# A graph attention kernel: self loops taken out of the edge lists, layer 2's sums split by columns between two engines, small tiles first

## The chip, the cores and the metric

The kernel runs on one core of a Trainium2 chip. The metric is the device time of one execution in microseconds (us), here the median of several runs. The profile comes from one more execution, taken by the hardware profiler. Engines are named as it names them: PE (matrix products; PEld loads their weights), DVE (vector engine), ACT (scalar engine), POOL (GpSimd), and SP, which here only issues transfers.

## What is computed

Two layers of graph attention over 10,000 nodes and 170,000 edges, then a final normalisation. All numbers are float32.

```python
src = concatenate([_s, _d, arange(10000)])      # 80000 random pairs, both ways, and one loop a node
dst = concatenate([_d, _s, arange(10000)])      # then both sorted by dst
def gat_conv(x, edge_index, W, a_src, a_dst, bias, heads, out_ch, concat):
    ei = _add_self_loops(edge_index, n)         # one more loop for every node
    xl = (x @ W).reshape(n, heads, out_ch)
    e = leaky_relu(alpha_src[src] + alpha_dst[dst], 0.2)
    e = exp(e - segment_max(e, dst)[dst])
    alpha = e / (segment_sum(e, dst)[dst] + 1e-16)
    return segment_sum(xl[src] * alpha[:, :, None], dst) + bias
h = relu(layer_norm(gat_conv(x, ..., heads=4, out_ch=256))) + (x @ Wr1 + br1)
h = layer_norm(gat_conv(h, ..., heads=1, out_ch=768)) + (h @ Wr2 + br2)
return layernorm(x + h)
```

The list of edges already holds a loop for each node, and the convolution adds another, so a node attends to itself twice.

## The kernel before, in words

There are three stages, and each handles the nodes in 79 tiles of 128, one node on each partition.

**Stage one** (lines 513 to 579) multiplies x by W1 tile by tile, adds each row's attention terms and writes it to a table in DRAM (`table1`, rows of 1032 numbers). In the same loop `prepare()` runs in small steps. It sorts the nodes by number of in-edges, most first, and builds `slots`: for tile t it has SLOTS[t] columns, each with one table row for every one of the tile's 128 nodes. `slot_counts()` (line 54) fixes these sizes ahead of the run, from the expected distribution of in-degrees with a margin of four standard deviations: `CAPS[t]` columns for the listed edges, and one in front for the added loop. A node with fewer edges gets the number of an empty row in the rest. If any tile had more edges than columns, `fits` would be zero and the program would take `general_path()`.

**Layer 1** (`ordered_layer1`, line 581) goes through the tiles from the most in-edges to the fewest. A `Ring` of 28 buffers is filled by indirect gathers on POOL (line 364), one a slot, 128 rows of 4 KB each. A gather into a buffer is issued once the slot before in that buffer has been consumed (`ring.fetch`, called after each slot). For a tile, `logits` (line 403) and `normalised` (line 420) turn the last columns of all its slots into softmax weights: small DVE operations with one exponential on ACT. The weighted rows are then summed into `acc` in PSUM, by three means:

- the first two slots (`ON_PE1`) by PE, with diagonal matrices that ACT makes from the weights (lines 616 to 629);
- of the others, every third by DVE alone, four operations of 256 columns (line 439);
- the rest by ACT, which multiplies the row in place (line 433), and DVE, which adds it in one operation of 1024 columns (line 435).

Between the slots of tile t stand the dense products: `deviation` and `scaled` (lines 468 and 480) normalise the sums of tile t-1 into h, `columns` (line 487) transposes h and x on PE, and `product` (line 145) multiplies h by W2 for layer 2's table, and x by Wr1 for the residual. The calls stand by hand: `events` has slot numbers at which `dense` and `next_x` are called. All PSUM results of products and transposes rotate through one pool of two buffers (`ps_big`). A tile with more slots than the ring has buffers (the first, 42) is done in three parts by `attend_parts` (line 442).

**Layer 2** (`ordered_layer2`, line 683) goes through the tiles in the same order, with rows of 770 numbers from `table2`, one head and a ring of 40. DVE alone sums the slots, one operation of 768 columns each (line 439). PE only makes the residual product (lines 740 and 742) from h1, which SP loads, and x, which POOL gathers. DVE normalises twice (lines 468 to 485 and 722 to 732), ACT does the last scaling (line 733), and POOL scatters the finished rows to the output (line 758). In each tile the steps stand in this order on DVE: the statistics and scaling of tile t-1, the weights of tile t, the final statistics of tile t-1, then the slots of tile t.

Each engine executes its own list of instructions in order, and waits where an operand isn't ready.

Of the kernel before, what the change touches and what calls it, by code (L numbers as in the profile page):

```python
# [26 lines left out]
F32 = mybir.dt.float32  # L28
# [5 lines left out]
P = 128  # L34
# [4 lines left out]
NO_NODE = 1 << 20  # L39
DEGREES = 64  # L40
# [3 lines left out]
RING2 = 40  # L44
ON_PE1 = 2
# [8 lines left out]
def slot_counts(n_nodes, n_edges):  # L54
# [8 lines left out]
    for t in range(-(-n_nodes // P)):  # L63
        room = t * P if t else 0.002
        k = next((k for k, m in enumerate(tails) if m + 4.0 * math.sqrt(m) * (t > 0) <= room), DEGREES - 3)
        counts.append(min(k + 1, DEGREES - 2))
# [4 lines left out]
def gnn_kernel(ctx, tc, x, x_cols, src, dst, src_col, dst_col, W1, a_src1, a_dst1, b1, g1, be1, Wr1, br1,  # L71
# [12 lines left out]
    SLOTS = [c + 1 for c in CAPS]  # L84
    FIRST = [sum(SLOTS[:t]) for t in range(NT)]
# [12 lines left out]
    ps_big = ctx.enter_context(tc.tile_pool(name="ps_big", bufs=2, space=PSUM))  # L98
    ps_tr = None

    @contextmanager
    def psum_for_transposes():

        nonlocal ps_tr
        with tc.tile_pool(name="ps_tr", bufs=2, space=PSUM) as ps_tr:
            yield
# [8 lines left out]
    slots = consts.tile([P, FIRST[-1] + SLOTS[-1]], I32, name="slots")  # L115
    order = consts.tile([P, NT], I32, name="order")
    fits = consts.tile([1, 1], I32, name="fits")
# [27 lines left out]
    def product(aT, w, n):  # L145

        k = w.shape[1]
        p = ps_big.tile([P, 2 * BANK], F32, name="big")
# [22 lines left out]
    def prepare():  # L171

        with tc.tile_pool(name="prep", bufs=1, side="right") as pool, \
# [144 lines left out]

            room = pool.tile([P, NT], F32, name="room")
            t = 0  # L320
            while t < NT:
                u = next((u for u in range(t, NT) if CAPS[u] != CAPS[t]), NT)
                nc.vector.memset(room[:, t:u], float(CAPS[t]))
                t = u
            nc.vector.tensor_sub(room, filled, room)
# [3 lines left out]
            yield  # L329
# [4 lines left out]


            def listed(t, window):
                k = CAPS[t]
                have = pool2.tile([P, CAPS[0]], F32, name="have")
                nc.vector.tensor_scalar(have[:, :k], node[:, :k], filled[:, t:t + 1], None, op0=OP.is_lt)
                got = pool2.tile([P, CAPS[0]], F32, name="got")  # L340
                nc.vector.tensor_scalar(got[:, :k], window[:, :k], float(-NP), None, op0=OP.add)
                nc.vector.tensor_mul(got[:, :k], got[:, :k], have[:, :k])
                nc.vector.tensor_scalar_add(slots[:, FIRST[t] + 1:FIRST[t] + 1 + k], got[:, :k], float(NP))
                nc.vector.tensor_copy(slots[:, FIRST[t]:FIRST[t] + 1], order[:, t:t + 1])

            asked = []
            for t in range(NT):
                k = CAPS[t]
                window = pool2.tile([P, CAPS[0]], I32, name="window", bufs=10)
                nc.gpsimd.indirect_dma_start(  # L350
                    out=window[:, :k], out_offset=None, in_=src,
                    in_offset=bass.IndirectOffsetOnAxis(ap=begin[:, t:t + 1], axis=0))
                asked.append((t, window))
                if t % 4 == 3:
                    for r in asked[:-4]:
                        listed(*r)
                    asked = asked[-4:]
                    yield
            yield
            for r in asked:  # L360
                listed(*r)
# [18 lines left out]
    class Ring:  # L380
# [6 lines left out]
        def fetch(self, upto):  # L387
            for q in range(self.issued, min(upto, FIRST[-1] + SLOTS[-1])):
# [31 lines left out]
    def normalised(small, e, heads):  # L420

        total = small.tile([P, heads], F32, name="total")
# [4 lines left out]

    def weigh(acc, row, e, dh, first=None, shared=False):

        if shared:  # L430
# [603 lines left out]
```

## Time and profile before

| what | us |
|---|---|
| median of 3 runs | 6468.38 (6455.11 to 6469.05) |
| profiled execution, its own time | 6474.16 |
| span in the profile | 6472.3 |
| DVE busy | 5053.9 (78%) |
| PE busy | 4198.2 (65%) |
| POOL busy | 3534.4 (55%) |
| ACT busy | 2688.0 (42%) |
| first gather of layer 1 at | 958.5 |
| first gather of layer 2 at | 3974.3 |

The profile gives the busy time of every engine, a table of the span in 40 equal slices, and groups of equal instructions with their number, their mean time and what ended the idle time before them. The trace behind it can be asked for any stretch: the instructions in order of time, the waits of an engine with what ended them, or a row of sums for a window. A line of the timeline has the start, the time taken, engine and line of code, operation, destination and sources, shapes and number, and in brackets the idle time before it with what ended it. The granted clock is PE's, as a share of full speed; the DMA share is the mean busy share of the core's 16 DMA engines. Issue times on POOL are about 0.95 us an indirect gather, with 0.30 between two.

### The profile page before, as it was taken

To read this page: it belongs to the slowest core of one execution; us is meant where nothing else is said; L and a number is where in the kernel's file an instruction comes from. 1 tells how busy PE (TensorE), PEld (TensorE's weight loads), DVE (VectorE), ACT (ScalarE), POOL (GpSimd) and SP (SyncE) were. 2 spreads that over 40 slices of the span, in tenths; PEclk is the share of its full clock that TensorE was granted. 3 is DMA by queue.
4 is the path that set the end of the run, shared out by engine and by line. 5 is a ranking of instruction groups with operands and counts; after the bars stand their busy time and mean duration, and the time that the engine had idled before them with its cause. 6 is when DMAs were issued, how large, how long until landed. Compare 5 with 4: busy or idle time off the path is not lost. (4 is left out here: it accounts for less than half of the span.)

```text
span 6472.3 us, 48744 instructions
## 1 busy us (share of the span) xinstructions
PE 4198.2 (65%) x11636; PEld 2278.5 (35%) x11636; DVE 5053.9 (78%) x8160; ACT 2688.0 (42%) x6591; POOL 3534.4 (55%) x3582
## 2 busy tenths in 40 slices
PE   8997982556766777778888996333434444445555
PEld 3443431333434444444455553111212222222332
DVE  5861426888888888888888884888878888888888
ACT  3433434666666666667666772011111111111111
POOL 3426534555555555555555553666666666666663
PEclk9999996778888888889899998666667777777777
DMA  4323237888888888888888885888878888888884
GB/s 140 122 76 70 93 106 287 289 293 315 299 301 301 303 304 297 300 295 299 293 299 307 308 312 180 277 281 288 281 272 287 282 280 281 279 286 283 279 291 161
DMA packets 459455, 1666.17 MB, mean 257 GB/s; under 512 B 105739, under 2 KB 109899, under 8 KB 459158
## 3 DMA queue, kind: packets, MB, share of 16 engines
q0 software_dynamic: 362176, 1486.59, 66.6%
q1 hardware_dynamic: 93168, 170.98, 7.8%
q10 hardware_dynamic: 3814, 5.39, 0.3%
q8 instruction: 94, 1.54, 0.1%
q14 instruction: 203, 1.66, 0.1%
HBM read 1516.88 MB, written 146.19 MB: 257 GB/s over the span
## 5 line engine op out<-in xcount | busy, mean ns | idle before, releaser
L364 POOL DMA_INDIRECT ring<-table,slots x2940 | 2789.2, 949 | 2161.4 <-DVE acc L439 889.7
L439 DVE SCALAR_TENSOR_TENSOR acc<-ring,e,acc 128x256 f32<-128x256 f32 (+1 forms) x3248 | 2332.4, 718 | 363.5 <-PE acc L625 201.5
L433 ACT ACTIVATE ring<-ring,e 128x256 f32<-128x256 f32 x3400 | 1390.8, 500 | 0.0
L435 DVE TENSOR_TENSOR acc<-acc,ring 128x1024 f32<-128x1024 f32 x850 | 1048.0, 1233 | 91.9 <-ACT ring L433 2.6
L740 PE MATMUL big<-wr,ident 128*128 128x512 f32 (+1 forms) x316 | 206.7, 745 | 1280.2 <-DMA wr<-in_x_dram,order 633.2
L742 PE MATMUL big<-w,wr 128*128 128x512 f32 (+1 forms) x2528 | 950.4, 531 | 23.1 <-issue 23.0
L625 PE MATMUL acc<-ring,diagonals 128*128 128x256 f32 x1248 | 424.3, 514 | 698.9 <-ACT diagonals L619 586.8
L152 PE MATMUL big<-w,hT 128*128 128x512 f32 (+1 forms) x2528 | 840.2, 490 | 56.8 <-ACT hT L494 56.8
L152 PE MATMUL big<-w,xT 128*128 128x512 f32 x1896 | 833.4, 601 | 55.8 <-DMA xT<-in_x_cols_dram 34.7
L152 PE MATMUL big<-wr,xT 128*128 128x512 f32 x1896 | 829.5, 594 | 0.7 <-ACT xT L494 0.7
L742 PEld LDWEIGHTS big<-w,wr 128*128 128x128 f32 x2528 | 531.3, 210 | 468.1 <-issue 432.6
L477 ACT ACTIVATE sd<-mv,eps 128x1 f32<-128x1 f32 x237 | 69.7, 294 | 1358.1 <-issue 585.4
L152 PEld LDWEIGHTS big<-w,hT 128*128 128x128 f32 x2528 | 471.9, 189 | 411.8 <-issue 289.1
L625 PEld LDWEIGHTS acc<-ring,diagonals 128*128 128x128 f32 x1248 | 326.9, 269 | 782.7 <-ACT diagonals L619 598.2
L152 PEld LDWEIGHTS big<-w,xT 128*128 128x128 f32 x1896 | 363.3, 193 | 522.9 <-issue 501.8
L740 PEld LDWEIGHTS big<-wr,ident 128*128 128x128 f32 x316 | 69.7, 249 | 1349.3 <-issue 449.3
L152 PEld LDWEIGHTS big<-wr,xT 128*128 128x128 f32 x1896 | 360.8, 190 | 423.4 <-issue 417.7
L417 ACT ACT_TABLE_LOAD x156 | 200.1, 1283 | 717.7 <-DVE e L416 636.7
L569 DVE TENSOR_TENSOR scr<-big,as_b 128x1024 f32<-128x1024 f32 x79 | 96.7, 1224 | 441.2 <-ACT row L566 426.3
L574 POOL TENSOR_TENSOR row<-row,none 128x1024 f32<-128x1024 f32 x79 | 187.0, 2368 | 334.9 <-ACT row L566 334.3
L572 ACT ACTIVATE scr<-scr 128x256 f32<-128x256 f32 x632 | 253.4, 402 | 122.2 <-DVE scr L569 118.3
L477 ACT ACT_TABLE_LOAD x157 | 201.4, 1283 | 229.7 <-DVE mv L475 149.5
(146 smaller groups left out, 3359.3 us busy)
## 6 DMA issues: line engine op xcount, KB each, us to landing
ring<-table,slots POOLq DMA_INDIRECT x2940
table<-row SPq DMA_DIRECT2D x79, 516.0 KB
h_d<-hT SPq DMA_DIRECT2D x79, 512.0 KB
wr<-h_d SPq DMA_DIRECT2D x79, 512.0 KB
xT<-in_x_cols_dram SPq DMA_DIRECT2D x79, 384.0 KB
w<-in_W_dram SPq DMA_DIRECT2D x6, 512.0 KB
w<-in_W_dram SPq DMA_DIRECT2D x1, 3072.0 KB
wr<-in_Wr_dram SPq DMA_DIRECT2D x1, 3072.0 KB
```

The costliest lines, as they stand in the source:

```text
L152: nc.tensor.matmul(p[:, c:e], aT[:, j, :], w[:, j, c:e], start=(j == 0), stop=(j == k - 1))
L364: nc.gpsimd.indirect_dma_start(out=to, out_offset=None, in_=table, in_offset=bass.IndirectOffsetOnAxis(ap=index, axis=0), **more)
L417: nc.scalar.activation(e, e, AF.Exp)
L433: nc.scalar.activation(row[:, s], row[:, s], AF.Copy, scale=e[:, h:h + 1])
L435: nc.vector.tensor_add(acc[:, :c], acc[:, :c], row[:, :c])
L439: nc.vector.scalar_tensor_tensor(acc[:, s], row[:, s], e[:, h:h + 1], (acc if first is None else first)[:, s], op0=OP.mult, op1=OP.add)
L477: nc.scalar.activation(sd, mv[:, 1:2], AF.Sqrt, bias=eps)
L572: nc.scalar.activation(m[:, s], m[:, s], AF.Copy, accum_out=row[:, C1 + i * H1 + h:C1 + i * H1 + h + 1])
L574: nc.gpsimd.tensor_add(row[:, :C1], row[:, :C1], b1_b)
L625: nc.tensor.matmul(acc[:, c:d], diagonals[:, k * H1 + i, :], ring.slot(FIRST[t] + k)[:, c:d], start=(k == 0 and c % BANK == 0), stop=(k == ...
L740: nc.tensor.matmul(r[:, c:d], ident, xt[:, c:d], start=True, stop=False)
L742: nc.tensor.matmul(r[:, c:d], hT[:, j, :], wr2[:, j, c:d], start=False, stop=(j == K1 - 1))
```

## The change

- The node's own loop is found in its list on the chip (`listed`) and taken out; the slot in front stands for both loops, and its weight is multiplied by `loops`, which is 2 where a loop was listed. A tile has one slot less.
- `slot_counts` uses a slightly smaller standard deviation.
- The tiles run from the fewest in-edges to the most, in both layers.
- Layer 1: of the rows after the first two, one in four and not one in three is summed by DVE alone (`SHARE`). The weights, diagonals and first two PE slots of tile t+1 are made during the last three slots of tile t (`LEAD`), where the ring can hold it. ACT's multiplication is issued three slots ahead. The pool `ps_big` becomes one buffer for the transposes and the product by W2, and one for the residual.
- Layer 2: DVE sums columns 0 to 511, and PE columns 512 to 767, into a PSUM tile of its own, with a diagonal from ACT for each slot. The weights are made ahead there too. Only the first tile's rows are asked for before the loads of biases and weights, and the product with br1 moves into the first tile.

The core of the diff (`prepare()` has the new lists first; the sizes, the order and the layers follow):

```diff
+BIG_SLOT = 4096.0
+LEAD = 3
+ON_PE2 = 512
+SHARE = 4
-        k = next((k for k, m in enumerate(tails) if m + 4.0 * math.sqrt(m) * (t > 0) <= room), DEGREES - 3)
+        k = next((k for k, m in enumerate(tails)
+                  if m + 4.0 * math.sqrt(m * (1.0 - m / n_nodes)) * (t > 0) <= room), DEGREES - 3)
-    SLOTS = [c + 1 for c in CAPS]
-    FIRST = [sum(SLOTS[:t]) for t in range(NT)]
+    SLOTS = CAPS
+    FIRST = [sum(SLOTS[t + 1:]) for t in range(NT)]
...
+            def listed(t, window):
+                m, k = window.shape[1:]
...
+                nc.vector.tensor_tensor(eq, window, named[:, t:t + m, None].to_broadcast(v), op=OP.is_equal)
+                nc.vector.tensor_mul(eq, eq, have)
+                nc.vector.tensor_mul(eq, eq, far[:, None, :k].to_broadcast(v))
+                nc.vector.tensor_reduce(loop[:, t:t + m], eq, axis=AX.X, op=OP.min)
...
+            nc.vector.tensor_scalar(loop, loop, 0.0, None, op0=OP.is_lt)
+            nc.vector.tensor_scalar_add(loops, loop, 1.0)
...
-    def normalised(small, e, heads):
+    def normalised(small, e, heads, t):
+        doubled(e, t)
...
+    def doubled(e, t):
+        nc.vector.tensor_scalar(e[:, 0], e[:, 0], loops[:, NT - 1 - t:NT - t], None, op0=OP.mult)
+    def multiply(row, e, dh):
+        for h in range(e.shape[1]):
+            s = slice(h * dh, (h + 1) * dh)
+            nc.scalar.activation(row[:, s], row[:, s], AF.Copy, scale=e[:, h:h + 1])
...
+    SLOTS, FIRST = SLOTS[::-1], FIRST[::-1]
...
     def ordered_layer1():
+                tc.tile_pool(name="ps_h1", bufs=1, space=PSUM) as ps_big, \
+                tc.tile_pool(name="ps_r1", bufs=1, space=PSUM) as ps_r, tc.manual_schedule():
             ring = Ring(pool, table1, R1, RING1)
-            ring.fetch(RING1)
+            ring.fetch(SLOTS[0])
...
+            def shared(k):
+                return (k - ON_PE1) % SHARE > 0
...
+                if full is not None:
+                    store(t - 2)
+                moves = []
+                if live:
+                    xT = pool.tile([P, K0, P], F32, name="xT")
+                    moves = columns(xT, xs[t])
+                multiplied(ON_PE1 + 2)
...
+                if whole and t + 1 < NT and SLOTS[t + 1] + LEAD <= ring.size:
+                    ahead = weights_of(t + 1)
+                for k in range(n if whole else 0):
+                    multiplied(k + 1 + LEAD)
+                    if k >= n - LEAD:
+                        ready += itertools.islice(ahead, 1)
+                    if k >= ON_PE1:
+                        weigh(acc, ring.slot(FIRST[t] + k), e[:, k], DH1, shared=shared(k))
+                    ring.fetch(FIRST[t] + k + 1 + ring.size)
+                    due(k)
...
     def ordered_layer2():
+            def sums(t, acc, e):
+                n = SLOTS[t]
+                nc.tensor.matmul(acc, ones, b2_b[0:1, ON_PE2:], start=True, stop=False)
+                for k in range(n):
+                    if k == n // 2:
+                        yield
+                    if k % G == 0:
+                        diagonals = pool.tile([P, G, P], F32, name="diagonals", bufs=2)
+                    nc.scalar.activation(diagonals[:, k % G, :], ident, AF.Copy, scale=e[:, k, :])
+                    nc.tensor.matmul(acc, diagonals[:, k % G, :],
+                                     ring.slot(FIRST[t] + k)[:, ON_PE2:C2], start=False, stop=(k == n - 1))
...
+                    stats = deviation(small, [a for m in means for a in pieces(m, C2 - ON_PE2)])
+                    next(tail, None)
+                    scaled(h, means, stats, g2_b, be2_b)
                     nc.vector.tensor_add(h, h, r[:, :C2])
-                if whole:
-                    normalised(small, e, H2)
-                if last:
-                    mean, inv = deviation(small, h, C2)
+                    mean, inv = deviation(small, pieces(h, C2 // 2))
                     o = pool.tile([P, C2], F32, name="out")
+                for _ in tail:
+                    pass
...
-                            weigh(acc, ring.slot(FIRST[t] + k), e[:, k], DH2, None if k else b2_b)
+                        weigh(acc, ring.slot(FIRST[t] + k), e[:, k], ON_PE2, None if k else b2_b)
...
+                        if not t and k == n - LEAD:
+                            nc.vector.tensor_add(be2_b, be2_b, q[:, :C2])
+                        if t + 1 < NT and k == n // 2:
+                            ins[t + 1] = fetch_x(t + 1)
```

## The prediction, made before the changed kernel ran

> **What bounds the kernel now.** I read the table of slices first, then the windows, to cut the 6472.3 us span into stages: node products and edge lists (0 to 958), layer 1 (first ring gather 958.5, its big tile until 1081, 78 ordinary tiles until 3942, drain until 3974), layer 2 (first gather 3974.3, big tile until 4090, 78 tiles until 6452.5, end). The columns of a window: its length, busy us of PE, PEld, DVE, ACT, POOL, granted clock, DMA share, GB/s.
>
> ```profile
> 970.00:1040.00 70.00, 15.73 (x36) 7.42 (x36) 33.35 (x59) 26.91 (x69) 36.38 (x40) 0.57 0.81 306
> ...
> 2000.00:2500.00 500.00, 367.00 (x1118) 215.94 (x1118) 428.25 (x660) 341.00 (x820) 262.82 (x279) 0.85 0.86 302
> ...
> 5000.00:5500.00 500.00, 226.29 (x576) 121.48 (x576) 419.54 (x649) 70.39 (x96) 324.31 (x338) 0.72 0.83 283
> ```
>
> DVE leads in both layers, at 85%. The timeline of single tiles says why. Layer 1, one turn of three rows and the end of a tile:
>
> ```profile
> 2402.25 2.06 DVE L439 SCALAR_TENSOR_TENSOR acc<-ring,e,acc 128x256 f32<-128x256 f32 x4
> 2404.42 2.57 DVE L435 TENSOR_TENSOR acc<-acc,ring 128x1024 f32<-128x1024 f32 x2
> 2407.03 2.06 DVE L439 SCALAR_TENSOR_TENSOR acc<-ring,e,acc 128x256 f32<-128x256 f32 x4
> ...
> 2409.49 10.46 PE L152 MATMUL big<-wr,xT 128*128 128x512 f32 x24
> ...
> 2435.16 2.06 DVE L439 SCALAR_TENSOR_TENSOR acc<-ring,e,acc 128x256 f32<-128x256 f32 x4 [2.72 <-PE acc L625]
> ```
>
> From start to start, a row that DVE weighs alone takes 2.17 us (2404.42 - 2402.25), a row that ACT has multiplied 1.305 (half of 2407.03 - 2404.42). The tile of 19 slots lasts 2397.48 to 2435.16, 37.7 us: 27.1 of rows, 10.6 fixed, of which 2.7 is the wait for the two slots that PE sums. That wait is in all 78 tiles:
>
> ```profile
> DVE acc L439 <- PE acc L625: 201.5, 78, 3.8
> DVE total L423 <- ACT e L417: 14.7, 66, 0.5
> DVE e L409 <- DMA ring<-table,slots: 13.0, 8, 5.4
> ```
>
> So DMA hardly holds layer 1 back, and PE does only through that wait, and in the smallest tiles (11 to 12 slots last 26.6 us, which is PE's own work). In layer 2 a slot costs 1.03 us of DVE, and a tile 7.3 more (18.7 us for 11 slots, 19.7 for 12, at the end). But while gathers run, DVE also stands still in places that no dependency explains:
>
> ```profile
> 4488.63 0.15 DVE L718 TENSOR_TENSOR ad<-ring,lift 128x1 f32<-128x1 f32 x1
> 4490.89 0.20 DVE L409 TENSOR_TENSOR e<-ring,ad 128x23 f32<-128x23 f32 x1 [2.10 <-remote]
> 4492.29 0.18 DVE L169 SCALAR_TENSOR_TENSOR e<-e 128x23 f32<-128x23 f32 x1 [1.20 <-DVE e L409]
> 4493.69 0.18 DVE L413 TENSOR_REDUCE new<-e 128x1 f32<-128x23 f32 x1 [1.22 <-issue]
> ```
>
> Such gaps over 0.25 us sum to 301 us in layer 2, 3.9 a tile, in one or two clusters every two tiles; the last tiles, without gathers, have none. Check of this reading: 78 x 7.3 + 1428 slots x 1.03 + 301 = 2341, against 2362.
>
> **What the change takes away, part by part.**
>
> *Slots.* Without the listed loop (its weight is doubled instead) and with the narrower margin of counts, the formula gives 1377 slots a layer, not 1470; the largest tile 41, not 42; the other 78 hold 1336, not 1428. So 93 gathers a layer go, at 1.25 us of POOL each (0.95 and 0.30 until the next).
>
> *Lists, stage one.* Some 400 small DVE operations become 20 groups of ten wider ones. PE is busy 867 of the first 970 us, DVE 484, and the steps still number fewer than the 79 tiles: zero, covered by PE. Uncovered it would be 20 x 10 x 0.35 = 70, less the 80 it replaces: also about zero.
>
> *Layer 1, DVE.* Of 1180 rows on DVE, one in four is now weighed alone, not one in three: 325 x 2.17 + 855 x 1.305 = 1821. The fixed part loses the wait for PE (2.7), since the next tile's weights, diagonals and two PE slots are made during the last three rows, and gains one 128x4 product (0.2, as L424): 10.6 - 2.7 + 0.2 = 8.1, x 78 = 632. Sum 2453, against 2861 measured for the same stretch.
>
> *What is late next in layer 1.* PE. Its work is 0.8 and 1.0 of transposes, 10.5, 10.6 and 3.6 of matmuls: 26.6. One PSUM buffer now serves the transposes and the product for layer 2, so the transposes of x wait for ACT's copy of that product, and those of h for ACT's move of x, about 1.4 more: a floor of 28. Tiles up to 14 slots (20 of them) fall below it; raising each to 28 adds 81. ACT multiplies 3/4 of the rows at 1.66 us: 27 us in a tile of 17 with its diagonals, table loads and copies, against DVE's 31, so it stays beside. The moved logits make two new waits. DVE stands at the doubled slot until ACT's exponential and its table load (1.28 and 0.25) are done, behind one row's addition: 0.4 a tile, 31; the last two rows queue behind it, and so do the next gathers. And the logits, three rows earlier, need the next tile's last row, which in a ring of 28 is only fetched when slot 2n-29 of this tile is free: for n=24 two rows (3 us) earlier. I take 2 us for the 28 tiles from 19 slots on, about 60; bounds 0 and 5 us a tile (140). Layer 1's tiles: 2453 + 81 + 31 + 60 = 2625, a gain of 236.
>
> *DMA.* Layer 1 moves 831 MB after (1377 x 0.528, and 1.31 a tile). The initial fill runs at 414 GB/s for 35 us (window 965 to 1000): 2030 us. The Trainium skill (DMA: Bandwidth & Descriptors, "Where 436 GB/s comes from") speaks against this: it has HBM bind at about 358 a core, which would make 2320. The row decides, but by either DMA stays under 2625; by the page 88% full, which is why I keep the 60.
>
> *Small tiles first.* Layer 1 begins after 8 gathers and the rows of x, not 28: first work at about 972, not 1004. The big tile (75; before 77) and the drain (32) now come last. First gather of layer 2: 972 + 2625 + 75 + 32 = 3704, before 3974.
>
> *Layer 2, DVE.* 512 of 768 columns stay. From 256 columns at 0.54 and 768 at 1.03, 512 columns take 0.785. The fixed part: three bn_stats of 256 for two of 384 (+0.17), one more piece in the scaling (+0.13), the doubling (+0.2), and the square root now comes after the exponential, so its table load is waited for (+0.6): 8.4. 78 x 8.4 + 1336 x 0.785 = 1704. The unexplained gaps stay at 3.9 a tile, since a tile has as many DVE instructions (44, before 41) and DMA runs no less; bounds 0 and 6.
>
> *Layer 2, POOL.* n + 2 gathers and scatters at 1.25: 1865 in the 78 tiles. POOL was under DVE and is now beside it. By tile the larger of 8.4 + 0.785n + 3.9 and 1.25(n+2), summed, is 2021 (11 tiles POOL's). With no gaps it is 1873 (69 tiles POOL's), with 6 us 2173. DMA moves 646 MB, 1580 us at 410.
>
> *Layer 2, PE and ACT.* PE gets n+1 matmuls of 256 columns (0.45, as L625's), beside 12.0 of residual: 19.6 for n=16, 1572 in all at full clock: covered by DVE and POOL. ACT gets n diagonals at 0.30; its final scaling stands behind them, but only the store needs that. The tile fetched one ahead, not two, has half a tile to land.
>
> *Ends of layer 2.* Before, weighing began 62 us after the first gather, behind bias loads and a product. Now the first tile needs 8 rows, but adds that product's result before its last three slots, so I let it end after 61. Then 2021 - 19, the big tile 60 (41 x 1.03 and its merging; before 55), and 26 of tail: 2149.
>
> Sum: 3704 + 2149 = 5853 of span, 10% less. The profiled execution took 6474.16, 1.9 over its span, and the median of the runs is 6468.38, 6 less: 5850.
>
> **The rivals.** (a) *The gaps of layer 2 go*, if they come from a backlog of gathers that POOL, now the bound, no longer builds. POOL's 1.25 then sets 69 tiles: 148 less, 5700. For: no gaps without gathers. Against: DMA share stays near 0.9. (b) *Layer 1 becomes a chain through the one PSUM buffer*: ACT's copy, ahead of the multiplies in ACT's queue, waits for PE, the multiplies and so DVE behind it. A floor of 33 instead of 28 adds 177: 6030. For: PE is at 94% in the last tiles of layer 1. Against: two accumulators and a full tile of slack. (c) *Slower*: PE's clock stays at half in layer 2, now that its matmuls come in groups paced by ACT. The Trainium skill (TensorE: Matmul & The Clock Gate, Part 1) has an idle window of about 3.4 us halve the clock, and layer 2's window above grants 0.72 as it is. 2 x 1572 = 3144 replaces 2002: 6990. It decides where PE's mean clock falls under 1572 / (2002 + 620) = 0.60. Against: PE would be busy some 80%, and 94% busy had 0.99. (d) *It doesn't do what it says*: a tile with more edges than its slots would send the program down the general path, far slower; the margin of four deviations makes that remote.
>
> **How the numbers follow.** Main case 5850 (0.52), its own range 5740 to 5960 from half of each bound; gaps gone 5700 (0.20); chain 6030 (0.20); gate or fallback, slower (0.04); the new waits eat all within 0.2%, about what a measurement can tell from no change (0.01); the rest (0.03) a few per cent faster. Range 5640 (gaps gone and no ring waits) to 6120 (chain, and gaps of 5). Faster 0.95, same 0.01, slower 0.04.
>
> **What would show it.** Right: no DVE wait for PE's accumulator from tiles of 15 slots up; small tiles of layer 1 at 28 us with PE over 0.9; layer 2's slots at 0.785; POOL gathers 1.25 apart in its large tiles; layer 2 starting near 3700. Wrong: DVE in layer 1 waiting on the ring or on ACT's multiplied rows for over 2 us a tile; PE's clock under 0.6 in layer 2; its gaps well off 3.9.

## The result and the profile after

The changed kernel takes 6207.40 us (median of 4 runs, 6204.62 to 6209.96), the kernel before 6461.89 beside it: a ratio of 0.961, 95% interval 0.9593 to 0.9628. The forecast had the direction right and the size wrong: 5850 was predicted, with a range of 5640 to 6120. The profiled execution has a span of 6208.2 us.

| stage | predicted | measured | difference |
|---|---|---|---|
| first gather of layer 1 at | 958 | 969.5 | +11 |
| from there to the first gather of layer 2 | 2746 | 2696 | -50 |
| first gather of layer 2 at | 3704 | 3665.9 | -38 |
| layer 2 to the end | 2149 | 2542 | +393 |

So layer 1 came out near its sum, and layer 2 is where the time went. All of the gain is layer 1's: before, it took 3016 us and layer 2 took 2498, so layer 2 became 44 us longer although it has 93 gathers fewer. The windows say it too. They are the second and third window that were shown of before, with the same columns:

```profile
2000.00:2500.00 500.00, 437.52 (x1359) 253.34 (x1358) 462.16 (x696) 419.85 (x1006) 306.30 (x311) 0.95 0.92 336
5000.00:5500.00 500.00, 368.24 (x1131) 237.37 (x1130) 322.33 (x647) 149.89 (x375) 303.05 (x315) 0.82 0.78 264
```

In layer 1 DVE rose from 86% busy to 92%. In layer 2 it fell from 84% to 64%, and nothing else took its place: PE is at 74%, POOL at 61%. Such a window has no engine that bounds it; something waits. DVE's waits in layer 2 name the place (columns: us in total, times, longest; `remote` is a wait that a semaphore update ended for which the trace names no instruction close by; a name is that of the record that ended last before the update, and can be another than the one waited for):

```profile
DVE wr L857 <- remote: 500.0, 53, 17.4
DVE wr L857 <- PE sum L821: 193.4, 23, 11.1
DVE be L892 <- PE big L161: 36.9, 1, 36.9
DVE wr L534 <- remote: 24.7, 10, 3.7
DVE wr L534 <- issue: 14.8, 8, 3.0
```

L857 is the addition of the residual, `tensor_add(h, h, r[:, :C2])`, once a tile. It stands 698 us in all. The 36.9 us at L892 are the first tile's wait for the product with br1. The gaps that the prediction carried over from before (301 us in many places) have all but gone: of them 44 us are left, at L534.

L857 needs two things: the line before it on DVE, and the last product of the residual, on PE. An engine tells the others that a step is done by updating a semaphore; such an update is called its signal here. This is one turn (from one L857 to the next), PE first:

```profile
4811.46 3.62 PE L832 MATMUL big<-w,wr 128*128 128x256 f32 x16
4815.00 0.69 PE L814 MATMUL sum<-b,ones 1*128 1x256 f32 x2
4815.63 2.86 PE L821 MATMUL sum<-ring,diagonals 128*128 128x256 f32 x12
4819.12 0.38 PE L821 MATMUL sum<-ring,diagonals 128*128 128x256 f32 x1 [0.63 <-issue]
4821.91 0.58 PE L821 MATMUL sum<-ring,diagonals 128*128 128x256 f32 x1 [2.42 <-DMA ring<-table,slots]
4824.02 1.50 PE L821 MATMUL sum<-ring,diagonals 128*128 128x256 f32 x2 [1.52 <-issue]
```

then DVE, SP and POOL in the same stretch:

```profile
4814.37 1.02 DVE L534 SCALAR_TENSOR_TENSOR wr<-wr,sd,be 128x768 f32<-128x768 f32 x1
4824.92 0.95 DVE L857 TENSOR_TENSOR wr<-wr,big 128x768 f32<-128x768 f32 x1 [9.54 <-remote]
```

```profile
4824.91 0.32 SPq L794 DMA_DIRECT2D wr<-h_d  x1
```

```profile
4820.52 1.02 POOL L900 DMA_INDIRECT out_dram<-out,order  x1 [0.30 <-issue]
4828.54 0.97 POOL L393 DMA_INDIRECT ring<-table,slots  x1 [6.99 <-DVE acc L476]
```

The residual's last product (L832) ends at 4815.1 by the records, and DVE is ready at 4815.4. DVE and SP start 9.5 us later, in the same instant, 4824.9. SP's load overwrites the buffer that the residual has read, and so waits for the very same signal of PE: two engines agree that PE's word came at 4824.9. So it is in 76 of the 79 tiles: SP's load and L857 start 0.01 us apart. The semaphore updates in the trace agree as well: none of PE's is recorded between 4810.7 and 4824.7, then twelve in 0.8 us. Twelve is the number of PE's steps with a signal whose records end between 4812.4 and 4825.6; the third of them is the residual's last product, and the third update stands at 4824.90. The first eleven come 0.04 to 0.10 us apart, where two such steps of PE lie 0.43 us apart at the least; so most of these products were done before their signals came. And PE itself, which had run ahead, crawls from 4818.5 on, one record every 0.7 to 2.8 us. All that ends 3.4 us after POOL's run of issues, back to back since 4798, has ended (4821.5).

So a turn is: 3.6 us from L857 to the first gather, n+1 times 1.25 until the last of POOL's n+2 issues starts, then 4.4 us until the held signal comes: 3.6 + 22.5 + 4.4 = 30.5 for these 17 slots. The first term is 3.6 in every turn, the last 3.5 to 5.6 (4.3 in the median of the turns between 4100 and 6050). The sum had taken the larger of POOL's run (23.8) and DVE's work with its gaps (21.7 + 3.9). In fact POOL's run and some 7 us in which POOL issues nothing stand in series. Over 78 tiles, 3.6 + 1.25(n+1) + 4.3 makes 2385 us (an estimate from these medians), against the 2021 of the prediction's maximum: 364 of the 393.

**The trace of before showed it already.** There, too, SP's load of h1 waits for the residual's last product:

```profile
4607.76 8.70 PE L742 MATMUL big<-w,wr 128*128 128x512 f32 x16
4616.30 0.59 PE L740 MATMUL big<-wr,ident 128*128 128x256 f32 x2
4616.73 3.62 PE L742 MATMUL big<-w,wr 128*128 128x256 f32 x16
```

```profile
4639.64 0.32 SPq L704 DMA_DIRECT2D wr<-h_d  x1
```

The product ends at 4620.3; the load starts 19.3 us later. Over 77 tiles that distance is 8.1 us in the median and 39 at most, and for long stretches it alternates between under 7 and over 14. DVE hardly felt it, since the addition came a whole tile after the product. The prediction did not look at SP's queue, which had time to spare.

The Trainium skill (Perfetto Trace Analysis, "Per-engine timelines") says how this can hide: the end of a product in the trace is an estimate from its size, and PE's signal goes out when PSUM has acknowledged the write. The trace agrees that the two can lie apart: an end at 4815.1, a signal at 4824.9. Whether the writes, their acknowledgement or the signal was held, no run here shows.

### The profile page after: what moved, and what is told of

It reads as the page before. It is cut to its first block, busy times and chain, and to the rows that moved or that the text cites. A ratio compares the mean times of both kernels' runs of the same rounds, so it can differ in the third digit from the quotient of the medians.

```text
span 6208.2 us, 56641 instructions
## 1 busy us (share of the span) xinstructions
PE 4880.9 (79%) x14464; PEld 2832.4 (46%) x14464; DVE 4437.2 (71%) x7872; ACT 3137.9 (51%) x8061; POOL 3388.6 (55%) x3396
## 5 line engine op out<-in xcount | busy, mean ns | idle before, releaser
L393 POOL DMA_INDIRECT ring<-table,slots x2754 | 2617.3, 950 | 1968.1 <-DVE acc L476 792.4
L476 DVE SCALAR_TENSOR_TENSOR acc<-ring,e,acc 128x256 f32<-128x256 f32 (+1 forms) x2606 | 1609.0, 617 | 143.0 <-PE acc L670 50.0
L465 ACT ACTIVATE ring<-ring,e 128x256 f32<-128x256 f32 x3536 | 1437.0, 505 | 0.0
L821 PE MATMUL sum<-ring,diagonals 128*128 128x256 f32 x2672 | 865.8, 477 | 559.2 <-issue 285.6
L821 PEld LDWEIGHTS sum<-ring,diagonals 128*128 128x128 f32 x2672 | 626.5, 241 | 794.3 <-issue 393.1
L832 PE MATMUL big<-w,wr 128*128 128x512 f32 (+1 forms) x2528 | 851.6, 488 | 27.8 <-issue 27.7
L832 PEld LDWEIGHTS big<-w,wr 128*128 128x128 f32 x2528 | 480.0, 190 | 372.4 <-issue 338.6
L820 ACT ACTIVATE diagonals<-ident,e 128x128 f32<-128x128 f32 x1336 | 417.2, 387 | 458.3 <-remote 297.8
L670 PE MATMUL acc<-ring,diagonals 128*128 128x256 f32 x1248 | 355.7, 449 | 305.1 <-ACT diagonals L665 273.0
L857 DVE TENSOR_TENSOR wr<-wr,big 128x768 f32<-128x768 f32 x79 | 75.4, 954 | 698.4 <-remote 500.0
```

The lines of the kernel that those rows point to most:

```text
L393: nc.gpsimd.indirect_dma_start(out=to, out_offset=None, in_=table, in_offset=bass.IndirectOffsetOnAxis(ap=index, axis=0), **more)
L465: nc.scalar.activation(row[:, s], row[:, s], AF.Copy, scale=e[:, h:h + 1])
L476: nc.vector.scalar_tensor_tensor(acc[:, s], row[:, s], e[:, h:h + 1], (acc if first is None else first)[:, s], op0=OP.mult, op1=OP.add)
L670: nc.tensor.matmul(acc[:, c:d], diagonals[:, k * H1 + i, :], ring.slot(FIRST[t] + k)[:, c:d], start=(k == 0 and c % BANK == 0), stop=(k == ...
L820: nc.scalar.activation(diagonals[:, k % G, :], ident, AF.Copy, scale=e[:, k, :])
L821: nc.tensor.matmul(acc, diagonals[:, k % G, :], ring.slot(FIRST[t] + k)[:, ON_PE2:C2], start=False, stop=(k == n - 1))
```

## The experiments

Theory: PE's completion signals are held back while layer 2's gathers are being issued, and a turn of layer 2 waits for them. Rivals: the order of PE's queue; the form or the amount of what is gathered; the column split itself. Each group of runs shared one chip and the runs of the kernel before (its time in brackets); from group to group the chip was another one, so that ratios compare better than times.

### First group (before: 6468.03)

**The first half of the sums after the addition.** On PE, these products stood behind the residual's last one and ran while the addition waited for it.

```diff
                     stats = deviation(small, [a for m in means for a in pieces(m, C2 - ON_PE2)])
-                    next(tail, None)
                     scaled(h, means, stats, g2_b, be2_b)
```

> Layer 2: the first half of a tile's column sums is issued only after the add of the residual, so that in TensorE's queue nothing stands between the residual's last product and the add's release. Theory (TensorE's signals are held back while layer 2's gathers are in flight): the add still starts only when the gathers of the tile have drained, VectorE still idles 400 to 700 us before it, and the whole stays at 6207, between 6170 and 6270. Rival (the sums queued behind the residual are what the add in fact waits for): the idle time before the add falls under 100 us and the whole to 5850 to 5950.

6318.41, ratio 0.9769 (0.9741 to 0.9797): slower than the changed kernel. DVE's waits in layer 2, where L856 is the addition:

```profile
DVE st L518 <- remote: 232.4, 32, 11.5
DVE wr L856 <- remote: 152.1, 20, 12.5
DVE wr L856 <- PE big L832: 150.1, 37, 7.9
DVE st L518 <- PE big L832: 89.8, 15, 10.8
DVE wr L856 <- PE sum L814: 67.9, 16, 8.8
```

The addition still waits 370 us, and the statistics over the sums 322 more: 692 together, against 681 in the changed kernel in the same stretch (3740 to 6130). The order of these products is not the cause. The theory did not fit wholly either: it had the addition wait 400 to 700 us and the whole at 6270 at most, as it did not see that the sums come late too.

**The residual between the two halves of the sums**, a turn earlier.

```diff
+                if live:
+                    r = residual(t)
                 for _ in tail:
                     pass
...
                 if live:
-                    r = residual(t)
                     if not t:
```

> Layer 2: the residual of a tile is issued between the two halves of its column sums, a whole turn before the add that needs it. Theory (signals held while gathers are in flight): the add finds its residual ready (idle under 100 us), but the sums' second half now runs in the time of the gathers and its signal is held instead, so that the statistics over the sums wait; the whole gains less than 150 us, 6060 to 6207. Rival (the residual is merely late in TensorE's queue): the wait is gone and nothing takes its place, 5820 to 5900.

6041.34, ratio 0.9341 (0.9313 to 0.9368), just under the theory's range. The addition waits no more, but DVE now stands elsewhere, 494 us at the correction of the weights:

```profile
DVE e L459 <- ACT e L446: 280.6, 38, 20.5
DVE e L459 <- issue: 213.8, 36, 10.3
```

ACT makes the exponential (L446) late: its queue has eight diagonals' room, and the ninth waits for PE, which is at the residual. These waits also let POOL run dry in mid-turn, and PE's signals can come through then (in the turn from 4707.2, POOL issues nothing from 4721.7 to 4725.7, and seven updates come at 4724.1 to 4724.6), before the gathers of the turn are over.

**Rows of 784 numbers** in layer 2's table, so `table2` and the ring have another row length.

```diff
-    table2 = dram.tile([NP + 1, R2], F32, name="table2")
+    R2W = 784
+    table2w = dram.tile([NP + 1, R2W], F32, name="table2w")
...
-            ring = Ring(pool, table2, R2, RING2)
+            ring = Ring(pool, table2w, R2W, RING2)
```

> The rows of layer 2's table are 784 numbers (3136 B) instead of 770 (3080 B), in DRAM and in the ring; 14 of them are filling that nothing reads. Theory that the held signals come from the form of these rows (layer 1, whose rows are 4128 B, shows no held signals): the wait before the add is gone and the whole comes to 5830 to 5900. Rival (the rows' length has nothing to do with it): 1.8% more bytes, 6207 to 6240, with 400 to 700 us of idle time before the add.

6226.17, ratio 0.9626 (0.9598 to 0.9654); the addition waits 681 us. The rows' length is innocent.

**Without the column split.**

```diff
-                    acc = ps_acc.tile([P, BANK], F32, name="acc")
-                    sum_ = ps_acc.tile([P, BANK], F32, name="sum")[:, :C2 - ON_PE2]
-                    tail = sums(t, sum_, e)
+                    acc = ps_acc.tile([P, 2 * BANK], F32, name="acc")
...
-                        weigh(acc, ring.slot(FIRST[t] + k), e[:, k], ON_PE2, None if k else b2_b)
+                        weigh(acc, ring.slot(FIRST[t] + k), e[:, k], C2, None if k else b2_b)
```

> Layer 2's column split undone: VectorE sums all 768 columns of every slot, TensorE only makes the residual; the order of the tiles, the self loop and layer 1 stay as in the changed kernel. Theory (the split bought nothing, since a turn is set by gathers, drain and the held signal): 6060 to 6210, so no slower than the changed kernel. Rival (the split does what it says and the lost time lies elsewhere): 1377 slots cost 0.25 us more each, 6480 to 6560.

6017.56, ratio 0.9304 (0.9277 to 0.9331), against 0.961 for the changed kernel. The split was not only worth nothing, as the theory had it (6060 to 6210), but a loss; in the fourth group, with both kernels on one chip, it was 204 us. The gain that is left comes from the rest of the change, which was not taken apart. Its window in layer 2:

```profile
4740.00:5240.00 500.00, 233.37 (x608) 126.12 (x606) 425.33 (x688) 72.58 (x100) 322.04 (x334) 0.73 0.84 281
```

DVE is back at 85%, with the short gaps of before.

### Second group (before: 6479.27)

What about the gathers holds the signals?

**A ring of 28 in layer 2.** `RING2 = 28` for 40.

> Only the length of layer 2's ring: 28 slots instead of 40. It is the partner of the run with rows of 1032 numbers, which has no room for 40. Theory (a tile's turn is gathers, drain and held signal in series, whatever the ring's length): 6190 to 6280, with 400 to 700 us of idle time before the add of the residual. Rival (a shorter ring means less traffic in flight and so less of the hold): the idle time under 300 us and the whole under 6150.

6227.32, ratio 0.9615 (0.9587 to 0.9643). The addition's wait fell to 448 us, within the theory's 400 to 700, and 241 us of waits for rows came in its place; the whole is as the theory has it.

**Rows of 1032 numbers, a ring of 28**: `R2W = 1032` in the kernel with wide rows.

> Layer 2's table has rows of 1032 numbers (4128 B, as in layer 1, whose gathers show no held signals), in a ring of 28; 262 numbers of each row are filling that nothing reads. The trace shows one row to a packet in layer 1 and two rows (6160 B) in layer 2. Theory that this form holds the signals: the idle time before the add falls under 100 us, the whole to 5850 to 5980. Rival (the form is innocent): it stays at 400 to 700 us, 6207 to 6350.

6230.28, ratio 0.9620 (0.9592 to 0.9648), as the ring of 28 alone. The wait at the addition is 386 us, a little under what the rival gave, with 310 for rows. Two rows to a packet (6160 B in the trace of the changed kernel) or one (4128 B here) makes no difference.

**Thin rows.**

```diff
+    RT = C2 - ON_PE2 + 2 * H2
+    table2t = dram.tile([NP + 1, RT], F32, name="table2t")
...
-            ring = Ring(pool, table2, R2, RING2)
+            ring = Ring(pool, table2t, RT, RING2)
...
-                        weigh(acc, ring.slot(FIRST[t] + k), e[:, k], ON_PE2, None if k else b2_b)
+                        half = C2 - ON_PE2
+                        two = ring.slot(FIRST[t] + k)[:, None, :half].to_broadcast([P, 2, half])
+                        nc.vector.scalar_tensor_tensor(
+                            acc.rearrange("p (a b) -> p a b", a=2), two, e[:, k],
+                            (acc if k else b2_b[:, :ON_PE2]).rearrange("p (a b) -> p a b", a=2),
+                            op0=OP.mult, op1=OP.add)
```

> Layer 2's gathers bring 258 numbers a row (1032 B) instead of 770: the columns that TensorE sums and the attention terms. VectorE's products read those 256 columns twice in place of the 512 that are left out, so that every engine has the same instructions of the same shapes; what is left out is the aggregation of 512 of the 768 columns (and, in the one tile over the ring, of 512 columns of its slots). Theory (it is the bytes in flight that hold TensorE's signals): with a third of them the gathers drain as they are issued, the idle time before the add falls under 100 us, the whole to 5820 to 5920. Rival (it is GpSimd's issuing of the gathers that holds them): the idle time stays over 400 us and the whole over 6150.

6200.71, ratio 0.9574 (0.9546 to 0.9602). The transfers fell to 117 GB/s, and the waits at the addition (L860 here) are all there, in layer 2 as a whole:

```profile
DVE wr L860 <- remote: 432.6, 47, 11.8
DVE wr L860 <- PE sum L824: 241.0, 27, 11.9
```

The theory that it is the bytes in flight fell with this run. What stayed the same is the number of gathers and their pace of 1.25 us on POOL. Nor is it their landing. From the end of POOL's last issue in a turn to the addition it is 3.3 us here, 3.1 in the changed kernel and 3.1 with rows of 4128 B (medians); from the end of the last packet of POOL's transfers it is +1.6, -0.1 and -1.6. The signals come some 3 us after the issuing ends, whether the rows are there or not.

That fits another row of the trace of the changed kernel. In layer 1 (1080 to 3500) POOL issues for 9.5 us at most with no more than the usual 0.30 between two issues, and PE's updates come 0.014 us behind the records' ends (median); in layer 2 it issues so for up to 36 us. But at layer 1's start, where it issues for 42 us (969 to 1012) with one gap of 0.7, PE's updates are up to 18 us late as well.

**Residual between, and room for 24 diagonals** (`bufs=6` for 2).

> The kernel with the residual between the halves of the sums, and room for 24 diagonals instead of 8, so that ScalarE makes all diagonals of most tiles without waiting for TensorE and reaches the exponential of the next tile in time. Theory (TensorE's signals held while gathers are in flight): the 494 us of waiting before the weights' correction vanish, but a turn now waits at the statistics over the column sums; 5940 to 6040. Rival (ScalarE's queue was all that was left): 5820 to 5900, with VectorE or GpSimd over 85% busy in layer 2.

6008.20, ratio 0.9277 (0.9250 to 0.9304), inside the theory's range. The wait for ACT fell to 124 us, and the statistics over the sums (L518) took it over with 342: where a turn needs PE's signal, there it stands.

### Third and fourth group (before: 6168.99, and 6452.32)

**Breaks in POOL's stream**: after every 4th or 8th gather of layer 2 a fill that nobody reads. The same is put into the kernel with the residual between, and into the one without the split.

```diff
                 self.issued = q + 1
+                if self.every and self.issued % self.every == 0:
+                    nc.gpsimd.memset(self.idle, 0.0)
```

> The changed kernel with one more instruction on GpSimd after every fourth gather of layer 2: a fill of a 128x1024 tile that nobody reads, about 1 us in which no gather is issued (half of the 2.37 us that the two-input add of that size takes in the first stage). 344 of them, some 340 us of extra work on GpSimd. Theory (TensorE's signals are held while gathers are issued without a break of a few us: layer 1, with breaks after 6 to 8 us, has none held, but its start, with 42 us of issuing without a break, has): the idle time before the add of the residual falls from 681 us under 250, and the whole gets faster in spite of the added work, 5990 to 6150. Rival (what is held waits for the gathers to land, whenever that is): the add waits as long or longer, 6450 to 6600.

> The same fill after every eighth gather: half of the added work, stretches of 10 us without a break. Theory (a break frees the signals): between the two, idle time before the add 200 to 450 us, the whole 6050 to 6200. Rival (gathers must land): 6330 to 6420.

> The residual between the halves of the sums, room for 20 diagonals, and the fill after every fourth gather. Theory: the 342 us of waiting at the statistics over the column sums fall under 120, and layer 2 is bound by GpSimd's gathers with their breaks; 5930 to 6030. Rival: the added work comes on top, 6200 to 6350.

> The kernel without the column split, with the fill after every fourth gather. It asks whether VectorE's own short gaps in layer 2 (some 15% of its time, waits for its own signals) are held signals too. Theory (yes): VectorE over 90% busy in layer 2 and 5950 to 6020 although GpSimd has 340 us more to do. Rival (VectorE's gaps are something else, or GpSimd becomes the bound): 6020 to 6250.

5969.76 (0.9678, 0.9650 to 0.9706), 5837.63 (0.9464, 0.9436 to 0.9491), 5979.06 (0.9693, 0.9665 to 0.9721) and 5985.76 (0.9704, 0.9676 to 0.9732). In all four the waits at the addition are gone (under 3 us), and PE's updates are 0.02 us behind its records to the 99th percentile. The first two are below the theory's ranges, the others inside them, although DVE is 88% busy in the last and not over 90. Taken for itself that seems to confirm the theory; but the kernel before, which has no breaks, took 6169 here, 300 less than in the groups before. The ratio of the kernel with four-gather breaks is worse than that of the changed kernel. So these runs say nothing of breaks: the chip was another one. That its 300 us are the prediction's 301 us of gaps is an inference; there is no trace of before from this chip. One row speaks for it: in the kernel without the split, DVE's waits for its own earlier steps in layer 2 (3740 to 5800) are 78 us in the first group and 0.5 here, though here with breaks.

Fourth group, with what each chip should show:

> The changed kernel unaltered, beside a kernel before that took 6169 on the chip of the last group and 6468 on the chips of the others. Theory (the held signals belong to the chip: where the kernel before takes 6169 there are none, neither its own 300 us of gaps in layer 2 nor the 681 us before the add of the residual): on a chip of the first kind (before near 6170) 5700 to 5800, a ratio of 0.925 to 0.94, TensorE's signals within 0.3 us of its products; on a chip of the second kind (before near 6470) 6207 again, a ratio of 0.96. Rival (the chip of the last group was faster for another reason): the ratio stays at 0.96 on either.

> The changed kernel with the fill on GpSimd after every eighth gather of layer 2. Where signals are held (before near 6470) by the theory that a break frees them: faster than the changed kernel beside it by 50 to 150 us, idle time before the add 200 to 450 us; by the rival that a break does nothing: slower by 120 to 210 us. Where none are held (before near 6170): slower than the changed kernel by 60 to 150 us, as GpSimd has 170 us more to do.

> Layer 2's column split undone, the rest of the change kept. Where signals are held (before near 6470): 6017 as before, faster than the changed kernel. Where none are held (before near 6170), by the theory that the held signals alone made the split a loss: slower than the changed kernel beside it, 5850 to 5920 against 5700 to 5800. Rival (the split loses by itself): faster than the changed kernel there too.

This chip had before at 6452.32 and is of the kind with late signals: 6203.68 (0.9616, 0.9600 to 0.9632), 6120.85 (0.9487, 0.9468 to 0.9505) and 5999.76 (0.9297, 0.9282 to 0.9313). With a break after every eighth gather the kernel is 83 us faster, though POOL has 172 fills of 0.97 us more to do, and the addition (L857, L860 with the breaks) waits 486 us instead of 636 in layer 2's main stretch (3740 to 5950). The unaltered kernel first:

```profile
DVE wr L857 <- remote: 441.2, 49, 11.8
DVE wr L857 <- PE sum L821: 194.8, 23, 11.1
```

```profile
DVE wr L860 <- remote: 367.6, 42, 12.5
DVE wr L860 <- PE sum L824: 83.9, 20, 7.8
DVE st L521 <- PE big L835: 41.0, 8, 12.0
DVE wr L860 <- PE big L835: 34.4, 10, 4.6
```

With the 41 us at the statistics, 527 us of waiting for PE are left. A break lets some signals through, but frees only a part, and the idle time stayed above the range that I gave.

### Fifth group (before: 6169.30)

> The changed kernel unaltered once more, for the chip of this group. Where the kernel before takes near 6170 and no signal of TensorE is late: 5700 to 5800, ratio 0.925 to 0.94. Where it takes near 6450 and signals are late: 6204, ratio 0.96.

> The fill on GpSimd after every fourth gather of layer 2. On a chip with late signals, by the theory that a break lets some of them through (a break after every eighth gather took 681 us of waiting down to 527 and the whole down by 83): 6040 to 6180, with under 450 us of idle time before the add. By the rival that only the end of the gathers frees them: 6280 or more, as 344 fills of 0.97 us lengthen each turn. On a chip without late signals: 5970, ratio 0.968.

And the time of a turn by its other term, one issue fewer: layer 1 stores the rows of x as it has them, and layer 2 loads them back on SP.

```diff
                     moves = columns(xT, xs[t])
+                    nc.sync.dma_start(x1_d[t], xs[t])
...
-                gather(xt, x[:, :], nodes(t))
+                nc.sync.dma_start(xt, x1_d[t])
```

> The kernel with the residual between the halves and room for 24 diagonals, and in addition layer 1 stores each tile's rows of x as it has gathered them, so that layer 2 reads them back with a plain load on SyncE and GpSimd has one issue fewer in a tile. On a chip with late signals, by the theory that a turn is GpSimd's issues (1.25 us each) plus a fixed drain: 79 issues fewer, 80 to 110 us off 6008, so 5890 to 5930 and the fastest of all on such a chip. Rival (a turn is bound by something else): 6000 to 6040, since layer 1 stores 0.4 MB more a tile. On a chip without late signals: 5560 to 5680.

This chip was a second one of the kind that the third group met. **The changed kernel, unaltered, takes 5723.49 here: ratio 0.9276 (0.9261 to 0.9292).** Its waits in layer 2 (3700 to 5500) and a window:

```profile
DVE e L459 <- ACT e L446: 142.9, 58, 5.9
DVE e L438 <- DMA ring<-table,slots: 56.4, 14, 8.5
DVE be L892 <- PE big L161: 23.4, 1, 23.4
...
DVE wr L857 <- PE big L832: 7.4, 4, 4.7
DVE wr L857 <- PE sum L821: 0.5, 1, 0.5
```

```profile
4740.00:5240.00 500.00, 418.53 (x1389) 289.01 (x1390) 398.53 (x795) 187.98 (x465) 382.01 (x388) 0.88 0.93 325
```

The addition waits 8 us instead of 698, to the end of the layer too, and PE's updates are 0.02 us behind its records. SP's load shows it as well. Here is the residual's last run of products, with the load that waits for it (and the next, merged into one line):

```profile
4783.16 3.62 PE L832 MATMUL big<-w,wr 128*128 128x256 f32 x16
4786.81 27.76 SPq L794 DMA_DIRECT2D wr<-h_d  x2
```

It starts 0.03 us after the product's end, and so does the load of each of the 77 tiles that wait for one; on the chip of the result it was 9.8 us in the median. POOL issues 388 times in 500 us, 1.29 apart: it is the bound now, as the prediction had it for the case without gaps. From 3853 to 5500 it never stops for more than 0.6 us, and yet no signal is late. The breaks cost time here: 5974.33 (0.9682, 0.9666 to 0.9698), 251 more than the unaltered kernel. With x kept, 5638.97 (0.9142, 0.9126 to 0.9157), the fastest of the group, and inside what was expected for such a chip; on a chip with late signals it was not tried.

| kernel | chips with late signals | chips without |
|---|---|---|
| before | 6452 to 6479 | 6169, 6169 |
| changed | 6204, 6207 | 5723 |
| without the column split | 6000, 6018 | not run |
| residual between, room for 24 diagonals | 6008 | not run |
| the same, with x kept | not run | 5639 |
| break after every 8th gather | 6121 | 5838 |
| break after every 4th gather | not run | 5970, 5974 |

The traces of the two kinds differ in one thing more. Where signals are late, records of updates are missing, in layer 1 too: in the changed kernel's trace 2841 of PE's 3453 and 4996 of DVE's 7452 are there. On the two other chips every trace has them all. So the recording itself may have a part in the lateness; no run here separates that.

## Why the prediction was wrong, by its own steps

**Right.** *Slots, rows and issues*: in layer 2 the twelve slots of one turn last 9.46 us, 0.788 each (0.785 predicted); POOL's gathers are 1.25 apart; in layer 1 a row by DVE alone takes 2.16 from start to start, three multiplied ones 3.95. *PE is late next in layer 1's small tiles*: tiles of up to 14 slots last 26.6 to 28.8 (28 predicted). *The new waits of layer 1*: for the exponential 39.0 us (31), for the ring's rows at the logits 41.4 (60). *The wait for PE's accumulator*, 2.7 in every tile, has shrunk to 50 us in 21:

```profile
DVE acc L476 <- PE acc L670: 50.0, 21, 7.1
DVE e L438 <- DMA ring<-table,slots: 41.4, 17, 6.2
DVE e L459 <- ACT e L446: 39.0, 61, 2.7
```

*DMA in layer 1*: the prediction's row decided over the 358 GB/s at which the Trainium skill (DMA: Bandwidth & Descriptors, "Where 436 GB/s comes from") has HBM bind. Rightly: this trace has 418 GB/s over the 13 us from 1806 to 1819.

**Wrong: "covered by DVE and POOL"**, of PE's work in layer 2. The work was of the size that the sum gave it, 12 us of residual and 0.43 a slot. But the sum counted when PE is done, not when the others learn of it: it put the wait for PE's signal at nothing. The change has DVE need two of PE's results in every turn, and on the chip of the result those signals come up to 20 us late while POOL issues gathers (at 6094 the residual's records end 19.9 us before L857 and SP's load start together). So the turn was not the larger of DVE's and POOL's work, but POOL's run and 7 us more, with 698 us of waiting at one line. The evidence was in the trace of before, on SP.

**Wrong in the same step: the gaps "stay at 3.9 a tile"**. They went down to 44 us in all; DVE now spends much of the time of the gathers waiting at the addition. 698 us more and some 260 of gaps less make 438, which accounts for the 393, with the rest of layer 2 some 45 below its sum.

**The rivals.** (a), *the gaps of layer 2 go*, 5700 us, has the number and the bound that the changed kernel shows on a chip without late signals, 5723 and POOL. But the prediction's reason, a backlog of gathers that is no longer built, is not what differs there: the chip does, and before is 300 us faster on it too. So that agreement is luck in part. On the chip of the result none of the four was it. (b), a chain in layer 1, did not come: layer 1 was 50 us under its sum. (c), PE's clock: 0.79 to 0.90 in layer 2, far from 0.60. The direction was right by layer 1 alone. The range ended at 6120 since no case had PE's signals in it.

**Open.** What makes the signals late, and why not on every chip. Shown is that the bytes, the row length, the ring's length and the order of the sums in PE's queue are not the cause, and that a short break helps in part. That it is POOL's unbroken issuing rests on where the late signals stand and when they end; on the fifth group's chip the same issuing makes none late, so there must be something else to it (on the third group's chip every kernel after the change had breaks). The recording of updates is one untested candidate, the number of gathers under way another. That the late signals account for the whole difference between the chips is likely, not shown: the kernel before was traced on one kind only. Where the first 11 us come from (the new lists of stage one are there) is open.

## What to carry to other kernels

An engine whose busy time is covered is not yet off the path: ask when its results are signalled, and look in the trace of before at every consumer of that engine, also at a queue that has time to spare, for the distance between a product's end and the start of what waits for nothing else. Where a consumer needs that signal in each turn, put a whole turn between the two (0.934 for 0.961 here), or leave the work on the engine that is there anyway: on a chip with late signals, not splitting the columns was 204 us faster than splitting them (5999.76 against 6203.68). And compare only with runs on the same chip: 300 us lay between chips for one and the same program, more than most edits were worth.

## What the hardware did that I had not expected

- From the recorded end of the residual's last product to SP's load that waits for its signal, it was 9.8 us in the median and 19.8 at most (77 loads, changed kernel), 9.6 and 20.7 when it ran again in the fourth group, and 0.03 in every one in the fifth.
- Late signals come in bursts: twelve updates in 0.8 us, some 0.04 us apart, after 14 us without any. In that turn PE's records run on at full speed for 6 us (4812.4 to 4818.5) while nothing is signalled, and then crawl, one in 0.7 to 2.8 us.
- Gathers of 1032 B a row take POOL the same 1.25 us as gathers of 3080 B: with a third of the bytes the ratio was 0.957 for 0.961.
- More work made a kernel faster: 172 fills of 0.97 us on POOL took 83 us off (6203.68 to 6120.85), where signals are late; where they are not, the kernel with the same fills took 114 more than the one without (5837.63 and 5723.49, on two chips with before at 6169).
